# A planner's other durations and due times: one instruction stream of a state-space and attention block, put in another order

## The chip, the cores and the metric

The kernel runs on one core of one Trainium2 chip. The metric is the device time of one launch in microseconds (us). The kernel before took 3198.13 us, the median of three runs (3196.02 to 3198.74).

## What is computed

All tensors are 32-bit floats. The input `x` has 8 images of 384 channels by 32x32 places. Layer 0 is a Mamba block, run forwards and backwards over the 1024 places, joined by a gated depthwise 3x3 convolution. Layer 1 is causal attention over the 1024 tokens (key width 64) and a feed-forward layer of width 1536 whose weights are Kronecker products. Cut to what matters:

```python
# layer 0, per image; mamba() runs forwards and on the flipped sequence
u, z  = split(x_norm @ in_proj_w.T)
u     = silu(causal_conv4(u) + conv1d_b)
dt, Bm, Cm = split(u @ x_proj_w.T)
delta = softplus(dt @ dt_proj_w.T + dt_proj_b)
h     = exp(delta * A) * h + (delta * u) * Bm      # a scan over 1024 places, 384 x 16 states
y     = (sum_n h * Cm + u * D) * silu(z)
g     = (mamba(x) + flip(mamba(flip(x)))) @ out_proj_w.T * scale_mod
x     = x + res_scale * (g + sigmoid(conv3x3(x_norm) + dw_b) * x_norm)
# layer 1
t = t + softmax(causal(rope(n @ Wq) @ rope(n @ Wk).T / 8)) @ (n @ Wv)   # n = layernorm(t)
t = t + gelu(layernorm(t) @ w_fc.T) @ w_proj.T
```

## The kernel before, in words

The work on an image is cut along the sequence into two halves of 512 places (`HB`). There are four scan steps for each image (`STEPS`): direction 1 on half 1, then on half 0, then direction 0 on half 0, then on half 1. A scan step has 12 *units*: six groups of 64 channels by two groups of eight states. So there are 48 units for each image and 384 in all. `scan` writes one unit as follows:

- SP (SyncE's DMA queue) loads four 256 KB tiles of `dd` (delta, spread over the states) into `dl`, and four of `db` (delta times u) into a tile of `hs`. The `hs` tiles are 128x2048, and there are five of them; `dl` has five tiles of 128x512.
- POOL (GpSimd) multiplies the `hs` tile by `br` (the input coefficients).
- ACT (ScalarE) makes four exponentials `da`, each in a PSUM bank. There are three such banks.
- DVE (VectorE) runs four `tensor_tensor_scan` of 128x512. In half of the steps each takes its first value from `carry`, a small tile that ACT copies out of the last scan of an earlier step.
- DVE multiplies the tile by `cb` (the output coefficients). In four units of twelve (`POOL_C`) POOL does that, with `cr`.
- PE (TensorE) sums over the states with four matmuls into the PSUM bank `y`. After four units ACT or DVE takes `y` away.

Everything else is *side work*, written as generators in small pieces: the norm and the input projection (`norm_in`), the 1-d convolution (`conv_tokens`, in which SP loads four overlapping copies `rep` and PE multiplies them by `cwt`), delta and its products (`prepare`), the gate and the 3x3 convolution (`gate`, `conv`, `local`, with `rep` and `cit`), the output projection (`project`), attention and the feed-forward layer. Their PSUM banks are the two `w`.

None of these calls issues an instruction. Each engine object records the call (`Plan.add`), and `Plan.order` then decides the order of all of them by list scheduling. It plays the program through with its own figures: `add` gives every instruction a duration `cost` (lines 149 to 173), `order` keeps a clock for each engine, and at every step the engine that can start first takes, of its operations that are ready, the one of lowest `rank`. Rank is the due time less a bonus (`rush`), and due times are counted in units: image b begins at 48b. A piece of side work gets its due time from `spread`, between two times of a table (FIRST, SECOND and OTHERS for layer 0; LAYER1, LAYER1_6 and LAYER1_7 for layer 1). The operations of a unit get theirs from SCAN. Buffers are handed out in the same play. The result is one fixed order for each engine; on the chip each engine works it off in order and waits for what it needs.

Three more parts of the play matter below. A load's landing time (lines 393 to 395) is made of a common rate and a fixed part, and the sync queue's clock is held back when more than 9 us of transfers are queued (`AHEAD`). `_gated` models TensorE's clock in windows of 3.413 us, with a half rate after a window of little work. `_fill` puts matmuls of zeros (`y<-zero,ident` in the profile) into modelled holes of TensorE until the last window is busy for the share `KEEP`. So the number of these fillers depends on the durations too; all other instructions are fixed.

All instructions are issued in `issue`, so in the profile they carry line 423, and the activation tables line 421. They are told apart by tile names. A 32-bit matmul appears as two records.

Of the kernel before, what the change touches and what calls it, by code (L numbers as in the profile page):

```python
# [34 lines left out]
POOL_END = (1, 3, 6, 8, 10)  # L35
TMP, SIDE = 5, 4
REPS = 4
RUSH = 3.54
START, LATER = -40.0, -8.0
LATER_US = 36.0  # L40


FIRST = (1.62, 3.88, 10.08, 14.37, 18.13, 22.35)
SECOND = (23.0, 0.55)
OTHERS = (4.41, 9.05, 14.9, 16.09, 22.99, 26.51, 31.92, 33.87, 42.68, 49.8)
BURST = 8.0
PROJECT = 1.86
LAYER1 = (39.24, 51.32, 61.95, 72.21, 83.3)
LAYER1_6 = (40.54, 50, 58.1, 65.96, 73.04)
LAYER1_7 = (39.38, 43.03, 45.9, 58.42, 62.69, 67.55, 71.01, 75.01, 81.01)  # L50
HASTE = 22.72
FREE = ["w", "da", "cb", "w", "da", "cb", "da"]
EXPS = 0.0
SCAN = (-1.59, -1.1, -0.46, -0.4, -0.36, 0.15, 0.79, 1.19)
class _Op:


    __slots__ = (
        "eng", "call", "args", "kw", "due", "rush", "seq", "cost", "tail", "bytes", "table", "batch", "tiles", "rank",
        "busy", "early", "succ", "left", "ready", "preds", "issued",  # L60
    )


# [13 lines left out]
class Plan:  # L77
# [5 lines left out]
        AF.Exp: "natural_log_exp_and_others", AF.Ln: "natural_log_exp_and_others",  # L83
        AF.Softplus: "softplus", AF.Silu: "silu_and_others", AF.Tanh: "silu_and_others", AF.Gelu: "gelu_and_others",
    }
    SWITCH = 1.3
    LOOSE = ("w", "tmp", "side")
    HURRY = 7.31
    PATIENCE = 1.81
    SETTLE = 0.2  # L90
    HOP = 0.18
    RATE = 300e3
    LAND = 2.54
    GATE = 3.413
    WARM, COLD = 0.8, 0.45
    KEEP = 0.65
    AHEAD = 9.0
    FAR = 1 << 24

    def __init__(self, nc, tc):  # L100
# [38 lines left out]
    def add(self, eng, call, method, args, kw):  # L139
        op = _Op()  # L140
        op.eng, op.call, op.args, op.kw = eng, call, args, kw
        op.due, op.rush, op.early, op.seq = self.due, self.rush, self.early, len(self.ops)
        outs = [args[0]] + [v for k, v in kw.items() if k == "accum_out"]
        ins = [v for v in args[1:] if isinstance(v, bass.AP)]
        ins += [v for k, v in kw.items() if k != "accum_out" and isinstance(v, bass.AP)]
        op.tiles = [(t, True) for t in outs] + [(t, False) for t in ins]
        n = max(math.prod(t.shape[1:]) for t in (outs[0], ins[0]) if len(t.shape) > 1) if ins else 1
        op.tail, op.bytes = self.HOP, 0
        op.table, op.batch = None, self.batch
        if method == "dma_start":  # L150
            op.bytes = math.prod(outs[0].shape) * 4
            op.cost = 0.45 if eng == "sync" else 1.0
        elif eng == "tensor":
            once = kw.get("is_transpose") or method == "transpose"

            m = outs[0].shape[0]
            rate = 1.05 if once else 0.62 if m <= 32 else 1.0 if m <= 64 else 1.72
            op.cost = 0.02 + rate * max(n, 96) / 1e3
            op.busy = 0.75 if once else min(1.0, ins[0].shape[0] / 96)
            op.tail += self.SETTLE  # L160
        elif eng == "vector":
            scan = method == "tensor_tensor_scan"
            op.cost = 0.14 + (2.09 if scan else 1.04) * n / 1e3
            if method == "scalar_tensor_tensor":
                op.cost += 0.06
            if method in ("tensor_copy", "bn_aggr"):
                op.cost = 0.16
        elif eng == "scalar":
            aps = sum(1 for k, v in kw.items() if k in ("scale", "bias") and isinstance(v, bass.AP))
            op.cost = 0.21 + 0.714 * n / 1e3 + 0.05 * (method == "activation") + 0.06 * aps + 0.2 * ("accum_out" in kw)  # L170
            op.table = self.SETS.get(args[2]) if method == "activation" else self.set
        elif eng == "gpsimd":
            op.cost = (0.45 + 1.0 * n / 1e3) if len(ins) == 1 else (0.1 + 2.165 * n / 1e3)
        self.ops.append(op)

    def spread(self, gen, a, e):
# [90 lines left out]
    def _fill(self, t, now, begun):  # L267

        work = sum(b * (e - max(s, now - self.GATE)) for s, e, b in self.ran[-40:] if e > now - self.GATE)
        out, left, right = self.nothing  # L270
        n = right.shape[1]
        made = []
        while work < self.KEEP * self.GATE:
            op = _Op()
            op.eng, op.call, op.args = "tensor", self.nc.tensor.matmul, (out, left, right)
            op.kw = dict(start=not begun, stop=False, skip_group_check=True)
            op.cost, op.busy, op.bytes, op.table = 0.02 + 1.72 * n / 1e3, 1.0, 0, None
            op.due, op.tiles, op.batch = 0.0, (), None
            if t + op.cost > now:
                break  # L280
            made.append((t, op))
            work += self._gated(t, op) - t
            t = self.ran[-1][1]
        return made

    def order(self):
# [11 lines left out]
        clock = dict.fromkeys(engines, 0.0)  # L298
        cand = {e: [op for op in self.ops if op.eng == e and not op.left] for e in engines}
        table, kept = None, 0.0  # L300
        drained = 0.0
        batches, whole = {}, {}
        for op in self.ops:
            if op.batch is not None and op.table is not None:
# [50 lines left out]
        while issued < total:  # L355
            best = None
            for e in engines:
                ts = [(at(op), op) for op in cand[e]]
                ts = [(t, op) for t, op in ts if t is not None]
                if not ts:  # L360
                    continue
                now = max(clock[e], min(t for t, _ in ts))
                if best is None or now < best[0]:
                    best = (now, e, ts)
            assert best, "no instruction can start"
            now, e, ts = best

            op = min((op for t, op in ts if t <= now), key=lambda op: op.rank)
            issued += 1
            cand[e].remove(op)  # L370
            op.issued = True
            for name in op.tiles:
                if name in self.slot:
                    continue
                tag = tag_of[name]
                self.slot[name] = min(free[tag])[1]
                free[tag].remove(min(free[tag]))
                queue[tag].remove(name)
            cost = op.cost
            if op.table is not None and op.table != table:  # L380
                cost += self.SWITCH
                table = op.table
            if e == "tensor" and self.nothing and now > clock[e]:

                y = [name for name in left_y if name in self.slot and users[name]]
                begun = bool(y) and left_y[y[0]] not in (0, all_y[y[0]])
                if begun or not y and max([last[n] for n in left_y if n in last], default=0.0) < clock[e]:
                    started += self._fill(clock[e], now, begun)
            started.append((now, op))
            end = clock[e] = self._gated(now, op) if e == "tensor" else now + cost  # L390
            done = end + op.tail
            if op.bytes:
                drained = max(drained, end + 0.3) + op.bytes / self.RATE
                done = drained + self.LAND
                clock[e] = max(end, drained - self.AHEAD)
            if op.table is not None:
                kept, batch = end, op.batch
                if batch is not None:
                    batches[batch] -= 1
            for name in op.tiles:  # L400
                users[name] -= 1
                if name in left_y and e == "tensor":
                    left_y[name] -= 1
                last[name] = max(last.get(name, 0.0), done)
                if not users[name]:
                    free[tag_of[name]].append((last[name], self.slot[name]))
            for o in op.succ:
                o.left -= 1
                o.ready = max(o.ready, end if o.eng == e and not op.bytes else done)
                if not o.left:  # L410
                    cand[o.eng].append(o)
        self.started = started
# [14 lines left out]
def conv_attn_kernel(  # L427
# [520 lines left out]
    def scan(b, si, lo=0, hi=HB):  # L948
# [38 lines left out]
        for k in range(n_u):  # L987
# [3 lines left out]
            if g == 0:  # L991
# [20 lines left out]
                if part == 0:  # L1012
# [7 lines left out]
                    for sb, (_, src) in zip(held_in, parts):  # L1020
                        plan.sync.dma_start(sb, src)
                    plan.due, plan.rush = t + 0.5 * f, RUSH
                    y = plan.tile(ps_y, [P, HB], "y")[:, :n]
# [22 lines left out]
            if save:  # L1046
                plan.due, plan.rush = t + f * 0.6, RUSH
                plan.scalar.copy(carry[:, k], hs[:, :, 0 if d else n - 1])
# [4 lines left out]
            else:  # L1053
                plan.vector.tensor_mul(hs, hs, cb[g].unsqueeze(1).to_broadcast([P, NQ, n]))
            plan.due, plan.rush = t + f * SCAN[7], RUSH
            done = part == 1 and g == SG - 1
# [417 lines left out]
```

## Time and profile before

| | |
|---|---|
| runs | 3196.02, 3198.13, 3198.74 us |
| span of the profiled execution | 3199.6 us (its own run time is not given apart) |
| granted TensorE clock, mean | 0.964 |
| VectorE busy | 2675.7 us, of which scans 1820 us |
| GpSimd busy | 2693.5 us, of which 128x2048 products 2256 us |
| ScalarE busy | 2189.8 us, of which exponentials 1057 us and table loads 205 us |
| TensorE busy, with fillers | 2770.0 us, of which fillers 350 us (1304 records) |
| DMA | 762 MB, mean 238 GB/s |

A wait row of the profile has, after the arrow's releaser, the total in us, how often, and the longest. A group row has busy time and mean duration; "DMA issues" end in the median us from issue to landing. A row of a timeline begins with start and length in us. Busy time is the union of the records, and neighbouring records on one engine may overlap by some hundredths of a us.

### The profile page before, as it was taken

To read this page: it belongs to the slowest core of one execution; us is meant where nothing else is said; L and a number is where in the kernel's file an instruction comes from. 1 tells how busy PE (TensorE), PEld (TensorE's weight loads), DVE (VectorE), ACT (ScalarE), POOL (GpSimd) and SP (SyncE) were. 2 spreads that over 40 slices of the span, in tenths; PEclk is the share of its full clock that TensorE was granted. 3 is DMA by queue.
4 is the path that set the end of the run, shared out by engine and by line. 5 is a ranking of instruction groups with operands and counts; after the bars stand their busy time and mean duration, and the time that the engine had idled before them with its cause. 6 is when DMAs were issued, how large, how long until landed. Compare 5 with 4: busy or idle time off the path is not lost. (4 is left out here: it accounts for less than half of the span.)

```text
span 3199.6 us, 39939 instructions
## 1 busy us (share of the span) xinstructions
PE 2770.0 (87%) x11855; PEld 1160.9 (36%) x11855; DVE 2675.7 (84%) x2740; ACT 2189.8 (68%) x3591; POOL 2693.5 (84%) x923
## 2 busy tenths in 40 slices
PE   7887888888988989899888888898898998787789
PEld 3323333343333334343333433334343433343345
DVE  3778778897898889997899978988799979998972
ACT  3566676867677776868578676767768686666564
POOL 2888887788998889889889888888898989998950
PEclk9998999999999999999999998999999999999899
DMA  7998997878979887887978788798878879665530
GB/s 232 289 293 259 285 286 224 260 230 260 265 229 279 250 248 242 270 251 239 266 239 268 237 252 249 223 279 243 262 236 258 259 237 279 196 197 175 174 100 12
DMA packets 424462, 762.47 MB, mean 238 GB/s; under 512 B 51020, under 2 KB 70804, under 8 KB 424244
## 3 DMA queue, kind: packets, MB, share of 16 engines
q1 hardware_dynamic: 424116, 759.80, 78.5%
q8 instruction: 93, 1.52, 0.2%
q14 instruction: 125, 1.02, 0.1%
q0 software_dynamic: 128, 0.11, 0.0%
HBM read 617.92 MB, written 141.80 MB: 237 GB/s over the span
## 5 line engine op out<-in xcount | busy, mean ns | idle before, releaser
L423 POOL TENSOR_TENSOR hs<-hs,br 128x2048 f32<-128x2048 f32 (+1 forms) x395 | 1737.6, 4406 | 312.6 <-PE y L423 156.1
L423 ACT ACTIVATE da<-dl,nega 128x512 f32<-128x512 f32 (+1 forms) x1584 | 1056.6, 677 | 534.5 <-DVE hs L423 384.0
L423 DVE TENSOR_TENSOR_SCAN hs<-da,carry,hs 128x512 f32<-128x512 f32 (+1 forms) x816 | 935.7, 1201 | 125.1 <-ACT da L423 113.7
L423 DVE TENSOR_TENSOR_SCAN hs<-da,hs 128x512 f32<-128x512 f32 x768 | 883.9, 1202 | 132.6 <-ACT da L423 115.5
L423 POOL TENSOR_TENSOR hs<-hs,cr 128x2048 f32<-128x2048 f32 (+1 forms) x137 | 599.0, 4372 | 30.1 <-DVE hs L423 23.3
L423 DVE TENSOR_TENSOR hs<-hs,cb 128x2048 f32<-128x2048 f32 (+1 forms) x259 | 574.1, 2217 | 44.4 <-ACT carry L423 38.4
L423 PE MATMUL y<-hs,sel 128*32 128x512 f32 (+1 forms) x3168 | 446.7, 607 | 91.2 <-POOL hs L423 54.5
L423 PE MATMUL y<-zero,ident 128*128 128x256 f32 x1304 | 349.7, 398 | 0.0
L423 PEld LDWEIGHTS y<-zero,ident 128*128 128x128 f32 x1304 | 237.9, 195 | 144.7 <-issue 121.4
L423 PE MATMUL w<-rep,cit 96*32 96x512 f32 x1152 | 199.2, 657 | 34.1 <-DMA rep<-xq 26.3
L421 ACT ACT_TABLE_LOAD x160 | 205.3, 1283 | 2.8
L423 PE MATMUL w<-v,p 128*128 128x384 f32 x546 | 196.5, 506 | 10.4 <-ACT p L423 9.3
L423 PEld LDWEIGHTS y<-hs,sel 128*32 128x32 f32 x3168 | 80.9, 110 | 339.3 <-DVE hs L423 128.6
L423 PE MATMUL w<-q,fc1s 128*128 128x512 f32 (+1 forms) x388 | 191.0, 607 | 12.8 <-ACT p L423 6.0
L423 PE MATMUL w<-rep,cwt 128*32 128x512 f32 x744 | 162.1, 613 | 28.8 <-DMA rep<-up 13.6
L423 PE MATMUL w<-wout,side 128*128 128x384 f32 x378 | 146.4, 515 | 31.7 <-DVE side L423 22.3
L423 ACT ACTIVATE uc<-w,vec 128x512 f32<-128x512 f32 x144 | 97.1, 680 | 109.4 <-PE w L423 91.4
L423 ACT COPY gl<-w 128x512 f32<-128x512 f32 (+2 forms) x254 | 136.7, 549 | 23.4 <-PE w L423 21.2
L423 PE MATMUL w<-xn,wz 128*128 128x512 f32 x288 | 135.5, 614 | 11.3 <-ACT uc L423 5.0
L423 PEld LDWEIGHTS w<-v,p 128*128 128x128 f32 x546 | 101.4, 194 | 100.3 <-ACT p L423 31.2
L423 PE MATMUL w<-xn,win 128*128 128x512 f32 x288 | 133.5, 605 | 4.6 <-ACT tmp L423 4.4
L423 PE MATMUL w<-wvs,gl 128*128 128x384 f32 x372 | 135.4, 502 | 0.8 <-ACT uc L423 0.6
(204 smaller groups left out, 3191.8 us busy)
## 6 DMA issues: line engine op xcount, KB each, us to landing
dl<-dd SPq DMA_DIRECT2D x744, 256.0 KB, 5.4
hs<-db SPq DMA_DIRECT2D x744, 256.0 KB, 5.6
rep<-up SPq DMA_DIRECT2D x180, 257.5 KB, 6.4
rep<-xq SPq DMA_DIRECT2D x192, 222.4 KB, 7.1
tmp<-in_x_dram SPq DMA_DIRECT2D x96, 256.0 KB, 5.4
dd<-tmp SPq DMA_DIRECT2D x96, 256.0 KB, 3.7
db<-uc SPq DMA_DIRECT2D x96, 256.0 KB, 4.2
br<-bd SPq DMA_DIRECT2D x62, 256.0 KB, 5.8
```

Of the source, the lines that this page charges most:

```text
L421: self.nc.scalar.preload_act_table_set(table)
L423: op.call(*args, **{k: self._bind(v) for k, v in op.kw.items()})
```

## The change

The diff leaves all calls that record work as they are, and with that the instructions, apart from fillers and the number of table loads that the order needs. It changes four things.

It replaces the formulas by which `add` prices an instruction. It gives each engine its own delay until another engine sees its result (`TAIL`), and a delay of 0.07 us to a later instruction of the same engine, but not on TensorE (`RAW`). It changes the play of transfers: a new rate, a fixed part for each (`FIX`), a lead of 1.2 us from the issue (`LEAD`), half a us less for writes to DRAM, and for the sync queue, in place of `AHEAD`, a limit of eight transfers in flight (`LANES`). It sets the due times, bonuses and `KEEP` anew. `op.done` is stored and not read by the functions shown.

```diff
-RUSH = 3.54
+RUSH = 3.67
-FIRST = (1.62, 3.88, 10.08, 14.37, 18.13, 22.35)
-SECOND = (23.0, 0.55)
-OTHERS = (4.41, 9.05, 14.9, 16.09, 22.99, 26.51, 31.92, 33.87, 42.68, 49.8)
-BURST = 8.0
-PROJECT = 1.86
-LAYER1 = (39.24, 51.32, 61.95, 72.21, 83.3)
-LAYER1_6 = (40.54, 50, 58.1, 65.96, 73.04)
-LAYER1_7 = (39.38, 43.03, 45.9, 58.42, 62.69, 67.55, 71.01, 75.01, 81.01)
-HASTE = 22.72
+FIRST = (2.5, 3.88, 9.91, 14.33, 18.07, 21.68)
+SECOND = (22.97, 0.53)
+OTHERS = (4.59, 6.98, 14.9, 16.45, 23.04, 25.93, 32.33, 33.23, 40.61, 49.8)
+BURST = 6.85
+PROJECT = 2
+LAYER1 = (39.92, 51.24, 61.95, 70.76, 83.52)
+LAYER1_6 = (39.47, 49.56, 58.33, 65.89, 73.37)
+LAYER1_7 = (41.09, 42.02, 49.22, 58.28, 64.49, 67.56, 67.85, 73.12, 81.01)
+HASTE = 22.26
-EXPS = 0.0
-SCAN = (-1.59, -1.1, -0.46, -0.4, -0.36, 0.15, 0.79, 1.19)
+EXPS = 0.09
+SCAN = (-1.38, -0.85, -0.52, -0.39, -0.37, 0.12, 0.79, 1.19)
...
-    SWITCH = 1.3
+    SWITCH = 1.4
-    PATIENCE = 1.81
-    SETTLE = 0.2
-    HOP = 0.18
-    RATE = 300e3
-    LAND = 2.54
+    PATIENCE = 1.92
+    TAIL = dict(tensor=0.21, vector=0.117, scalar=0.14, gpsimd=0.1, sync=0.1)
+    RAW = 0.07
+    RATE = 320e3
+    LEAD, FIX, LAND = 1.2, 0.1, 2.8
+    LANES = 8
-    KEEP = 0.65
-    AHEAD = 9.0
+    KEEP = 0.67
...
         if method == "dma_start":
             op.bytes = math.prod(outs[0].shape) * 4
-            op.cost = 0.45 if eng == "sync" else 1.0
+            op.write = outs[0].space == bass.MemoryType.DRAM
+            op.cost = (0.45 if op.write else 0.62) if eng == "sync" else 0.8
         elif eng == "tensor":
             once = kw.get("is_transpose") or method == "transpose"
             m = outs[0].shape[0]
-            rate = 1.05 if once else 0.62 if m <= 32 else 1.0 if m <= 64 else 1.72
-            op.cost = 0.02 + rate * max(n, 96) / 1e3
+            rate = 0.85 if once else 0.43 if m <= 32 else 0.84 if m <= 64 else 1.676
+            op.cost = rate * max(n, 64) / 1e3
-            op.tail += self.SETTLE
         elif eng == "vector":
-            scan = method == "tensor_tensor_scan"
-            op.cost = 0.14 + (2.09 if scan else 1.04) * n / 1e3
+            if method == "tensor_tensor_scan":
+                op.cost = 2.0833e-3 * n + (0.108 if isinstance(args[3], bass.AP) else 0.048)
...
+            else:
+                op.cost = max(0.07, 0.048 + 1.0417e-3 * n + 0.06 * len(small))
         elif eng == "scalar":
-            op.cost = 0.21 + 0.714 * n / 1e3 + 0.05 * (method == "activation") + 0.06 * aps + 0.2 * ("accum_out" in kw)
+            op.cost = 0.05 + 0.8333e-3 * n + 0.05 * (not psum) + 0.095 * aps + 0.09 * ("accum_out" in kw)
         elif eng == "gpsimd":
-            op.cost = (0.45 + 1.0 * n / 1e3) if len(ins) == 1 else (0.1 + 2.165 * n / 1e3)
+            op.cost = 0.2 if n <= 16 else 0.2 + 2.5e-3 * n if len(ins) == 1 else 0.14 + 2.119e-3 * n
...
             if op.bytes:
-                drained = max(drained, end + 0.3) + op.bytes / self.RATE
-                done = drained + self.LAND
-                clock[e] = max(end, drained - self.AHEAD)
+                drained = max(drained, now + self.LEAD) + op.bytes / self.RATE + self.FIX
+                done = drained + self.LAND - 0.5 * op.write
+                if e == "sync":
+                    lanes = lanes[1:] + [done]
+                    clock[e] = max(end, lanes[0])
+            op.done = done
...
-                o.ready = max(o.ready, end if o.eng == e and not op.bytes else done)
+                near = o.eng == e and not op.bytes
+                o.ready = max(o.ready, end + (0.0 if e == "tensor" else self.RAW) if near else done)
```

In `_fill` the price of a filler goes from 0.02 + 1.72n/1000 to 1.676n/1000 us, with n = 256.

More of the change, by code (lines that the diff above doesn't have):

```diff
@@ L59 @@
         "eng", "call", "args", "kw", "due", "rush", "seq", "cost", "tail", "bytes", "table", "batch", "tiles", "rank",
-        "busy", "early", "succ", "left", "ready", "preds", "issued",
+        "busy", "early", "write", "done", "succ", "left", "ready", "preds", "issued",
     )
@@ L147, in add @@
         n = max(math.prod(t.shape[1:]) for t in (outs[0], ins[0]) if len(t.shape) > 1) if ins else 1
-        op.tail, op.bytes = self.HOP, 0
-        op.table, op.batch = None, self.batch
+        op.bytes, op.table, op.batch = 0, None, self.batch
+        op.tail = self.TAIL[eng]
+        small = [v for v in args[1:] if isinstance(v, bass.AP) and len(v.shape) == 2 and v.shape[-1] == 1]
+        psum = bool(ins) and ins[0].space == bass.MemoryType.PSUM
         if method == "dma_start":
             op.bytes = math.prod(outs[0].shape) * 4
-            op.cost = 0.45 if eng == "sync" else 1.0
+            op.write = outs[0].space == bass.MemoryType.DRAM
+            op.cost = (0.45 if op.write else 0.62) if eng == "sync" else 0.8
         elif eng == "tensor":
@@ L156, in add @@
             m = outs[0].shape[0]
-            rate = 1.05 if once else 0.62 if m <= 32 else 1.0 if m <= 64 else 1.72
-            op.cost = 0.02 + rate * max(n, 96) / 1e3
+            rate = 0.85 if once else 0.43 if m <= 32 else 0.84 if m <= 64 else 1.676
+            op.cost = rate * max(n, 64) / 1e3
             op.busy = 0.75 if once else min(1.0, ins[0].shape[0] / 96)
-            op.tail += self.SETTLE
         elif eng == "vector":
-            scan = method == "tensor_tensor_scan"
-            op.cost = 0.14 + (2.09 if scan else 1.04) * n / 1e3
[L164 to L167, printed above, removed]
+            if method == "tensor_tensor_scan":
+                op.cost = 2.0833e-3 * n + (0.108 if isinstance(args[3], bass.AP) else 0.048)
+            elif method == "bn_stats":
+                op.cost = 0.157 + 1.0417e-3 * n
+            elif method == "bn_aggr":
+                op.cost = 0.1
+            elif method == "memset":
+                op.cost = 0.06 + 0.5e-3 * n
+            else:
+                op.cost = max(0.07, 0.048 + 1.0417e-3 * n + 0.06 * len(small))
         elif eng == "scalar":
             aps = sum(1 for k, v in kw.items() if k in ("scale", "bias") and isinstance(v, bass.AP))
-            op.cost = 0.21 + 0.714 * n / 1e3 + 0.05 * (method == "activation") + 0.06 * aps + 0.2 * ("accum_out" in kw)
+            op.cost = 0.05 + 0.8333e-3 * n + 0.05 * (not psum) + 0.095 * aps + 0.09 * ("accum_out" in kw)
             op.table = self.SETS.get(args[2]) if method == "activation" else self.set
         elif eng == "gpsimd":
-            op.cost = (0.45 + 1.0 * n / 1e3) if len(ins) == 1 else (0.1 + 2.165 * n / 1e3)
+            op.cost = 0.2 if n <= 16 else 0.2 + 2.5e-3 * n if len(ins) == 1 else 0.14 + 2.119e-3 * n
         self.ops.append(op)
@@ L276, in _fill @@
             op.kw = dict(start=not begun, stop=False, skip_group_check=True)
-            op.cost, op.busy, op.bytes, op.table = 0.02 + 1.72 * n / 1e3, 1.0, 0, None
+            op.cost, op.busy, op.bytes, op.table = 1.676 * n / 1e3, 1.0, 0, None
             op.due, op.tiles, op.batch = 0.0, (), None
@@ L300, in order @@
         table, kept = None, 0.0
-        drained = 0.0
+        drained, lanes = 0.0, [0.0] * self.LANES
         batches, whole = {}, {}
```

## The prediction

> **What bounds the kernel now.** I read the busy shares first, then the stretches, then the waits.
>
> ```profile
> PE 2770.0 (87%) x11855; PEld 1160.9 (36%) x11855; DVE 2675.7 (84%) x2740; ACT 2189.8 (68%) x3591; POOL 2693.5 (84%) x923
> ```
> ```profile
> core 0: us, PE busy (x) PEld busy (x) DVE busy (x) ACT busy (x) POOL busy (x), PEclk, DMA share, GB/s
> 0.00:160.00 160.00, 130.09 (x418) 54.62 (x419) 83.77 (x118) 75.12 (x113) 87.55 (x48) 0.94 0.88 260
> 160.00:400.00 240.00, 194.00 (x792) 73.65 (x790) 192.76 (x159) 147.93 (x221) 210.36 (x67) 0.92 0.93 279
> 400.00:2800.00 2400.00, 2112.52 (x9128) 865.55 (x9132) 2105.53 (x2084) 1722.55 (x2783) 2130.10 (x709) 0.97 0.83 251
> 2800.00:3080.00 280.00, 224.04 (x1004) 104.11 (x996) 249.24 (x293) 177.65 (x342) 249.14 (x85) 0.92 0.58 177
> 3080.00:3200.00 120.00, 109.37 (x524) 62.92 (x520) 44.45 (x90) 66.59 (x136) 16.39 (x17) 1.00 0.08 25
> ```
>
> DVE and POOL share the bound, each with about 500 us of holes. In 400 to 2800 they stand idle 294 and 270 us of 2400; the rest lies mostly at both ends, where too little work is ready. An order can mend the holes only. The waits tell who is late:
>
> ```profile
> ACT da L423 <- DVE hs L423: 384.0, 485, 5.2
> DVE hs L423 <- ACT da L423: 229.2, 91, 6.8
> POOL hs L423 <- PE y L423: 156.1, 49, 10.5
> ACT da L423 <- DMA dl<-dd: 117.7, 87, 5.0
> ACT uc L423 <- PE w L423: 94.5, 61, 5.7
> ```
>
> The first is harmless: ScalarE is ahead and waits for one of three `da` banks. The second is the damage: 91 times a scan had no exponential. ScalarE was then itself held up at the head of its queue, by the two last lines among others: a `dl` tile that had not landed, or a convolution's accumulator that TensorE had not finished. The third is `hs` buffers that come free late.
>
> [...] exponentials stand 229.2 us behind other work while the scans starve. So a wrong place in the queue costs time, and the place comes from the planner's prices. [...] the trace shows 0.92 in 2800 to 3080, where TensorE was 80% busy. [...] mean durations are not the spacing; this case's timeline shows it (next part). [...] Landings of `dl` from 3.0 to 8.9 us at 83% busy DMA engines fit a part that grows with load; the constants have none.
>
> **The prices, part by part.** The spacing is in the timeline:
>
> ```profile
> 1193.51 8.33 DVE L423 TENSOR_TENSOR_SCAN hs<-da,carry,hs 128x512 f32<-128x512 f32 x7
> 1251.83 3.43 DVE L423 TENSOR_TENSOR_SCAN hs<-da,hs 128x512 f32<-128x512 f32 x3
> 1208.78 2.76 PE L423 MATMUL w<-rep,cit 96*32 96x512 f32 x24
> 1227.20 1.92 PE L423 MATMUL y<-hs,sel 128*32 128x512 f32 x16
> ```
> ```profile
> dl<-dd SPq DMA_DIRECT2D x744, 256.0 KB, 5.4
> hs<-db SPq DMA_DIRECT2D x744, 256.0 KB, 5.6
> rep<-up SPq DMA_DIRECT2D x180, 257.5 KB, 6.4
> rep<-xq SPq DMA_DIRECT2D x192, 222.4 KB, 7.1
> ```
>
> Seven scans with a carry take 8.33, one 1.26: spacing (8.33-1.26)/6 = 1.18 us. Without a carry (3.43-1.20)/2 = 1.115. Old price 1.21 for both, new 1.175 and 1.115. The multiply by `cb` starts at 1191.30 and its follower at 1193.51: 2.21; old 2.27, new 2.18. A matmul is two records: the 12 of a convolution take 2.76; old 4.04, new 2.64. Four y matmuls alone take 1.06 and eight 1.92, so four add 0.86; old 1.35, new 0.88. POOL's 128x2048 hardly moves (4.53 to 4.48; record 4.54). A 256 KB load lands, by price, after 0.45+0.3+0.87+2.54 = 4.16 old and 1.2+0.82+0.1+2.8 = 4.92 new, against 5.4 to 7.1. SP's issue of a load is 0.45 old, 0.62 new; the four in a row that a `rep` or `dl` set needs start 0.56 to 0.65 apart. The eight lanes are new; SP does wait for its own landings (151 times for `hs<-db`, 64.3 us), so there is something for them to model. In sum the new prices are nearer the spacing on every engine but POOL, where both are right.
>
> What that moves, row by row, against the profiled span of 3199.6 (1.5 us, 0.05%, above the median 3198.13; what lies around the span is not shown):
>
> 1. **Late `dl`.** The landing is under-priced by 5.4-4.16 = 1.24 us before and 0.48 after, so 0.76 us better. Over 87 waits 66 us of ScalarE. Three `da` banks (3 x 1.18 us) can hide one such wait, not a row of them: I take half, **-33**. Bounds 0 (the load waits for one of five `dl` buffers anyway: SP stands 285 us behind ACT `da`) and -66.
> 2. **Late convolutions.** The same 0.76 plus three later issues of 0.17 makes 1.27 us for the last `rep`. Over 61 waits 77 us; half, **-39**. Bounds 0 and -77.
> 3. **Cheaper TensorE.** Summed over the counts of the groups, real matmuls are priced at about 2390 us before and 1960 after. Less assumed delay of y moves POOL's 49 waits either way: 49 x 0.47 = 23 us, taken as 0, bounds -23 and +23. But `_fill` adds fillers wherever its picture of TensorE is less than 67% busy. There are 1304/2 = 652 now. The 430 us that leave the picture could be filled by up to 1000 more; I take 330. A filler takes about 0.44 us (ten records 2.34). If a quarter stand before a matmul that was ready on the chip, and cost half of it: 330/4 x 0.22 = **+18**. Bounds: 0 where the array is idle as planned, below zero by the clock (mean 0.964: at most 3.6% of the TensorE part of the chain, PE 6% of the span, 7 us), and +102 as in the rival below.
> 4. **Dues.** POOL's products and exponentials come due 0.21 and 0.25 of a unit later (SCAN), EXPS gives 0.09 back. A unit is 3199.6/384 = 8.3 us. An extra PSUM copy of 0.58 before the exponentials in a quarter of the units would be 96 x 0.58 = 56, half of it seen by DVE: +28. The other end is -28, where the copy was what held TensorE's banks. Taken 0. Norms (OTHERS) and projections (PROJECT) move by up to 2 units; these have a whole batch to be hidden in: 0, and if that cover fails a 1.8 us join per batch, 14.
> 5. **Ends.** The first 160 us are limited by loads (DMA share 0.88) and the last 120 by a serial chain with PE 109 us busy. LAYER1_7 moves dues by up to 3.3 units; an order can't shorten the chain: 0, bounds -12 and +12.
> 6. **Table loads** (160 x 1.283 us; SWITCH 1.3 to 1.4, PATIENCE +0.11): ten fewer or more are 13 us on an engine busy 68%: 0.
>
> Sum -33-39+18 = -54: 3199.6-54 = 3145.6; on the median's footing **3144**.
>
> **The rivals.** (a) *As summed*, 3109 to 3185, chance 0.50. (b) *The queues fit throughout*: with spacing priced right the scheduler lines up all engines, and not only loads. If half of POOL's middle waits go (PE y 153, `db` 35, issue 32: half of 220 is 110) the time is 3199-110 = 3089. For it: the near-exact prices. Against it: landings stay under-priced, and most PE y waits may be five `hs` buffers rather than order. Chance 0.20. (c) *Buffers set the loads, whatever the order*: rows 1 and 2 are zero, 3192 to 3204. For it SP's 285 us behind `da` and 301 us behind y. It is also the rival that the new order differs little where it matters. Chance 0.09. (d) *Fillers crowd TensorE*, ending slower: 700 more, a third of them whole in front of y or convolution matmuls, 233 x 0.44 = 102 us; y late means `hs` late and POOL idle, and with the gain of 72 the end is 3199+30 = 3229. It decides from about 165 such fillers on. For it: PE is 87% busy already and its y products stand on POOL's longest wait. Against: fillers are put only in modelled gaps, and real TensorE work is priced lower there because it is shorter. Chance 0.21.
>
> **How the numbers follow.** About 0.2% (6 us) is what a measurement of this kernel tells from no change. Faster: (a), (b) and 0.02 of (c) give 0.72; same 0.07 from (c); slower (d) 0.21. The range 3085 to 3225 holds (a), (c), about half of (b) and half of (d): 0.80. The likeliest case's own range is 3109 to 3185.
>
> **What would show it.** Right: DVE `hs` behind ACT `da` falls from 229 to about 160, `da` behind `dl` from 118 to about 60, `uc` behind PE from 94 to about 50, middle DVE idle below 260 us of 2400. Filler records rise from 1304 to near 1960. Wrong in steps 1 and 2: these rows stay, or shrink with no gain while POOL behind PE y grows. Wrong in step 3: fillers above 2700 and PE y above 200 us, or fewer fillers than now. The prediction fails altogether if the ends, and not the middle, move the time.

## The result: slower by 1.8%, and the profile after

The changed kernel took **3254.86 us** (median of 4; 3250.05 to 3261.27) against 3197.07 for the kernel before in the same sessions (median of 4). The ratio is 1.0177, interval 1.0154 to 1.02. The forecast of 3144 had the wrong sign. The profiled execution of the changed kernel has a span of 3248.3 us, 48.7 more than the one before.

The page's first part, and the stretch from 400 to 2800 us, to be set beside the same lines of before:

```profile
PE 2993.6 (92%) x12775; PEld 1312.7 (40%) x12775; DVE 2656.8 (82%) x2740; ACT 2178.3 (67%) x3589; POOL 2689.1 (83%) x923
```
```profile
400.00:2800.00 2400.00, 2272.66 (x9712) 975.35 (x9709) 2041.93 (x2030) 1685.19 (x2733) 2084.71 (x698) 1.00 0.84 249
```

DVE, ACT and POOL do the same work as before, so their busy times hardly move. TensorE has 224 us more. In the middle, DVE and POOL are 64 and 45 us less busy than before in the same 2400 us: most of the loss is there. (In the first 400 us DVE does another 16 us less work than before; some of all this is made up after 2800.) At the start of the last scan (3169.0 us, before 3116.3) the changed kernel is 53 us behind. The waits of the changed kernel (total us, times, longest):

```profile
ACT da L433 <- DVE hs L433: 282.6, 379, 4.3
DVE hs L433 <- ACT da L433: 248.3, 101, 12.1
POOL hs L433 <- PE y L433: 178.6, 52, 7.4
ACT uc L433 <- PE w L433: 159.9, 111, 6.9
ACT v L433 <- PE w L433: 64.4, 41, 3.4
ACT da L433 <- DMA dl<-dd: 58.6, 48, 5.5
```

The wait for late `dl` loads fell from 117.7 to 58.6 us, as forecast. But `uc` behind TensorE rose from 94.5 to 159.9, `v` from 26.4 to 64.4. Over all rows of ScalarE's waits, those for a DMA went from 185 to 92 us, and **those for TensorE from 263 to 486**. One wait was traded for a larger one. But ScalarE is not the bound, so what VectorE waits for counts more. Over the whole span its waits for ScalarE rose from 307 to 343 us, over all rows, and its own **waits for TensorE from 111 to 171** (of these, 52 to 106 between 400 and 2800). The rows behind TensorE that grew most, first before, then after:

```profile
DVE side L423 <- PE y L423: 31.4, 14, 3.7
DVE p L423 <- PE w L423: 14.4, 3, 9.2
DVE q L423 <- PE w L423: 13.4, 10, 3.7
DVE sm L423 <- PE w L423: 11.7, 5, 5.3
```
```profile
DVE p L433 <- PE w L433: 39.0, 10, 7.4
DVE side L433 <- PE y L433: 38.7, 25, 4.4
DVE sm L433 <- PE w L433: 38.3, 33, 3.6
DVE q L433 <- PE w L433: 22.6, 14, 3.7
```

These are VectorE's parts of the gate and of layer 1. So more of the added idle time of VectorE comes straight from TensorE (60 us) than through ScalarE (36). Two groups of the page show what TensorE does with its extra time:

```profile
L433 PE MATMUL y<-zero,ident 128*128 128x256 f32 x2224 | 582.3, 393 | 0.0
...
L433 PE MATMUL w<-rep,cwt 128*32 128x512 f32 x744 | 219.8, 610 | 2.8 <-DMA rep<-up 1.9
```

There are 1112 fillers (2224 records) for 652, and the same 372 matmuls of the 1-d convolution take 219.8 us, before 162.1.

### The profile page after: what moved, and what is told of

The parts are those of the page before. It is cut to its first block, busy times and chain, and to the rows that moved or that the text cites. A ratio compares the mean times of both kernels' runs of the same rounds, so it can differ in the third digit from the quotient of the medians.

```text
span 3248.3 us, 41611 instructions
## 1 busy us (share of the span) xinstructions
PE 2993.6 (92%) x12775; PEld 1312.7 (40%) x12775; DVE 2656.8 (82%) x2740; ACT 2178.3 (67%) x3589; POOL 2689.1 (83%) x923
## 5 line engine op out<-in xcount | busy, mean ns | idle before, releaser
L433 POOL TENSOR_TENSOR hs<-hs,br 128x2048 f32<-128x2048 f32 (+1 forms) x395 | 1737.1, 4407 | 339.0 <-PE y L433 178.6
L433 DVE TENSOR_TENSOR_SCAN hs<-da,hs 128x512 f32<-128x512 f32 x768 | 886.7, 1204 | 156.1 <-ACT da L433 135.7
L433 PE MATMUL y<-zero,ident 128*128 128x256 f32 x2224 | 582.3, 393 | 0.0
L433 PE MATMUL y<-hs,sel 128*32 128x512 f32 (+1 forms) x3168 | 473.9, 600 | 98.5 <-POOL hs L433 55.1
L433 PEld LDWEIGHTS y<-zero,ident 128*128 128x128 f32 x2224 | 398.2, 191 | 259.4 <-issue 218.7
L433 PE MATMUL w<-rep,cwt 128*32 128x512 f32 x744 | 219.8, 610 | 2.8 <-DMA rep<-up 1.9
```

What stands on the lines that cost most here:

```text
L433: op.call(*args, **{k: self._bind(v) for k, v in op.kw.items()})
```

## Where the price is wrong

The old and the new price of a 32-column matmul are flat numbers, 0.337 and 0.22 us for an input of 128x512. Two pieces of TensorE's timeline, first of the kernel before, then of the changed one (start, length, records; two records are one matmul):

```profile
401.91 0.59 PE L423 MATMUL w<-rep,cwt 128*32 128x512 f32 x1
402.19 0.59 PE L423 MATMUL y<-hs,sel 128*32 128x512 f32 x1
402.34 0.59 PE L423 MATMUL w<-rep,cwt 128*32 128x512 f32 x1
```
```profile
436.12 2.56 PE L433 MATMUL w<-rep,cwt 128*32 128x512 f32 x12
438.62 0.70 PE L433 MATMUL y<-zero,ident 128*128 128x256 f32 x2
439.25 1.91 PE L433 MATMUL w<-rep,cwt 128*32 128x512 f32 x4
441.08 1.13 PE L433 MATMUL y<-side,ddiag 128*128 128x512 f32 x2
```

The two records of the convolution are 0.43 apart, so one matmul takes 0.86 by itself; here a record of y runs beside it. In the changed kernel six matmuls hold TensorE 2.50 us to the next start, 0.42 each; a filler stands between them and the last two; these hold it 1.83, **0.92 each**. The 3x3 convolution of 12 shown in the prediction had 0.23 each. The difference is the neighbour. In `conv_tokens` a set of four matmuls writes four different groups of 32 columns, one for each `rep` tile, while the two matmuls that one `rep` tile feeds (one for each direction) write the same group in two banks. Of the y run at 1227.20 us in the kernel before, the first four records start within 0.02 us, the first eight, those of four matmuls, within 0.47, and the next four matmuls begin 0.88 after the first. So in this trace partners on other columns are nearly free (0.88 us for four, 0.86 for one by itself), and a matmul without them costs a whole one. Four at 0.22 are right as a set and wrong one by one. When the four `rep` loads land one after another, the planner plays each matmul at 0.22, puts fillers or other work in between, and believes that TensorE is free four times sooner than it is.

The traces show how often that happens. Counting unbroken runs of the 1-d convolution on TensorE, the kernel before has 20 runs of eight matmuls and 4 runs of only two; the changed kernel has 3 of eight and **65 of two**. A run of two takes 1.83 us in the median there, 0.92 for each matmul, and a run of four 1.00, 0.25 for each. Of the 65, 48 have a filler right before or behind them. So the low price made the planner break up the sets that the low price needs.

Counted from the starts of the records (an instruction holds TensorE until the next start, or for its length less the 0.16 us by which neighbours overlap), all real matmuls held TensorE 2305 us before and 2312 after. So the real work took as long as before. The planner's prices for it, added up over every matmul of the two programs, are 2453 us before and 2008 after (the prediction's count by groups gave 2390 and 1960): 6% too high and 13% too low. Part of the held time passed at a half clock (the granted clock of the traces is 1 or 0.5, and was 0.5 for 229 us of the span before and 113 after), for which the planner adds by itself; counted at the full clock it is 2216 and 2279, and the sums are 11% too high and 12% too low. So by its sum neither table is the nearer one. They miss on opposite sides. The 372 matmuls of the 1-d convolution are priced at 125 us before and 82 after, and held TensorE 140 and 182.

## The experiments

Medians are over the runs of each kernel; the ratio is to the kernel before on the same chip. Beside the runs of the experiments the kernel before took 3196 to 3204 us. The last two columns are from the profiles: fillers (half the records), and ScalarE's waits for TensorE over all rows.

| kernel | us | ratio, interval | fillers | ACT waits for PE, us |
|---|---|---|---|---|
| before | 3197 | 1 | 652 | 263 |
| changed | 3255 | 1.0177 (1.0154, 1.0200) | 1112 | 486 |
| a_half | 3230 | 1.0082 (1.0062, 1.0101) | 556 | 450 |
| a_none | 3289 | 1.0267 (1.0247, 1.0287) | 0 | 503 |
| prices | 3347 | 1.0456 (1.0424, 1.0488) | 1150 | 505 |
| dues | 3229 | 1.0088 (1.0067, 1.0108) | 686 | 307 |
| a_pe | 3251 | 1.0160 (1.0136, 1.0183) | 638 | 276 |
| a_dma | 3291 | 1.0287 (1.0265, 1.0310) | 1069 | 491 |
| a_eng | 3293 | 1.0291 (1.0273, 1.0309) | 1149 | 495 |
| b_narrow | 3280 | 1.0250 (1.0204, 1.0296) | 862 | 391 |
| b_shift1 | 3248 | 1.0144 (1.0110, 1.0179) | 662 | 308 |
| a_shift1 | 3302 | 1.0317 (1.0276, 1.0358) | 1163 | 523 |
| a_later | 3327 | 1.0388 (1.0353, 1.0423) | 1112 | 444 |
| b_more | 3220 | 1.0064 (1.0039, 1.0090) | 1108 | 286 |
| b_pe | 3360 | 1.0514 (1.0494, 1.0535) | 1101 | 496 |
| a_pe_shift1 | 3248 | 1.0162 (1.0142, 1.0183) | 614 | 291 |
| a_pack | 3219 | 1.0081 (1.0052, 1.0111) | 923 | 355 |
| a_shift1_half | 3251 | 1.0178 (1.0157, 1.0199) | 582 | 471 |
| a_pack_half | 3243 | 1.0135 (1.0114, 1.0157) | 462 | 370 |
| b_less | 3210 | 1.0025 (1.0011, 1.0039) | 456 | 272 |

**First: fillers, prices or dues?** The theory was the prediction's rival (d), surplus fillers (F); against it the order of the real instructions (O), the dues (D), or a mixture of dues and prices that do not fit (M). `a_half` and `a_none` keep the changed order and only drop fillers where it is handed on (the diff is `a_none`'s; `a_half` leaves out every second one):

```diff
-        return [op for _, op in started]
+        return [op for _, op in started if not isinstance(op.tiles, tuple)]
```

> The changed kernel with its order kept, and every second filler matmul left out (about 556 left instead of 1112; before has 652; a filler multiplies zeros, so nothing that is computed is left out). Theory F (the added fillers delay TensorE): the time falls from 3255 most of the way back, to 3190-3225, ScalarE's uc wait for TensorE from 160 us to about 110, and POOL's wait for y from 179 to about 160. Theory O (the order of the real instructions is the cause): within 10 us of 3255. A third possibility is a drop of the granted clock that gives back what the fillers took.

> The changed kernel with its order kept and all fillers left out (nothing that is computed is left out). Theory F with a cheap clock: 3160-3200. Theory F with a costly clock: granted clock under 0.85 and 3220-3300, so that the fillers are needed. Theory O: 3245-3265 if the clock matters little.

Half of the fillers gone won 25 us, a little less than half of the loss and short of F's 3190 to 3225. `uc` behind TensorE fell to 129 us, not to 110; the other waits hardly moved. With none the granted clock falls to 0.902 (0.983 changed; the mark was 0.85) and the time rises to 3289. So F is right in part: the surplus costs, some fillers are needed, and some 30 us are left in this order that the count of fillers does not explain. `prices` is the changed kernel with the constants from RUSH to SCAN of before; `dues` is the reverse:

> The new prices, play of transfers, SWITCH, PATIENCE and KEEP, with the due times and bonuses of before. Theory F: the fillers come with the prices, so slower than before by at least 30 us, 3230-3260. Theory D (the dues set anew are what costs): 3190-3205. Theory M (the dues were fitted to the prices they stand with, and a mixture is worse than either): over 3265.

> The old prices and the old play with the due times and bonuses of the change. Theory F: 3190-3215, with about 650 fillers. Theory D: 3240-3260. Theory M: over 3215 with fillers as before.

Each half alone is slower than before, and prices alone are worst: 3347. The new dues take back about 90 of those 150 us, yet on the old prices they lose 0.88%, 28 us. So M holds, and the new prices look like the harmful half.

**Second: which price?** One group at a time is set back:

```diff
 # a_pe
-            rate = 0.85 if once else 0.43 if m <= 32 else 0.84 if m <= 64 else 1.676
-            op.cost = rate * max(n, 64) / 1e3
+            rate = 1.05 if once else 0.62 if m <= 32 else 1.0 if m <= 64 else 1.72
+            op.cost = 0.02 + rate * max(n, 96) / 1e3
-    TAIL = dict(tensor=0.21, ...
+    TAIL = dict(tensor=0.38, ...
...
 # b_narrow, in the kernel before
-            rate = ... 0.62 if m <= 32 else 1.0 if m <= 64 ...
+            rate = ... 0.40 if m <= 32 else 0.82 if m <= 64 ...
```

`a_dma` takes back the transfers and SP's prices, `a_eng` the formulas of VectorE, ScalarE and GpSimd with their delays:

```diff
 # a_dma
-    RATE = 320e3
-    LEAD, FIX, LAND = 1.2, 0.1, 2.8
+    RATE = 300e3
+    LAND, AHEAD = 2.54, 9.0
-            op.cost = (0.45 if op.write else 0.62) if eng == "sync" else 0.8
+            op.cost = 0.45 if eng == "sync" else 1.0
...
 # a_eng
-    TAIL = dict(tensor=0.21, vector=0.117, scalar=0.14, gpsimd=0.1, sync=0.1)
-    RAW = 0.07
+    TAIL = dict(tensor=0.21, vector=0.18, scalar=0.18, gpsimd=0.18, sync=0.18)
+    RAW = 0.0
...
```

> The changed kernel with TensorE's prices and its delay (0.38 us) of before, fillers' price included; the rest new. Theory P (TensorE priced too low: a 32-column matmul costs 0.22 only where its partners run beside it, and about 0.98 alone; so ScalarE's copies stand too early in its queue and fillers go in between partners): back to 3185-3215, fillers 600-800, ScalarE's waits for TensorE in all from 486 us to under 320. Theory Q (another price, or any new order is a draw): 3235-3270 or worse.

> The changed kernel with the play of transfers and SP's prices of before; the rest new. Theory P: no better than the change, 3245-3290, and ScalarE's wait for dl loads from 59 us back over 100. Theory T (the transfers' new play, with its eight lanes, is what costs): 3190-3220.

> The changed kernel with the prices and delays of VectorE, ScalarE and GpSimd of before and no RAW; the rest new. Theory P: 3240-3290, ScalarE's waits for TensorE still over 400 us. Theory E (the cheaper scans and exponentials are what costs): 3190-3220.

> The kernel before with one price changed: matmuls of 32 columns at 0.225 us for 512 (before 0.337) and of 64 at 0.44; all else as before, dues too. Theory P: slower than before, 3215-3260, fillers up from 652 to about 800, ScalarE's waits for TensorE from 263 us to over 350. Theory Q: any value, with no tie to ScalarE's waits for TensorE. If this price does nothing: 3190-3207.

TensorE's prices did to the fillers and to ScalarE's waits exactly what theory P said (638 and 276 us), and P's time failed: 3251, not 3185 to 3215. Taking back any other group left the waits at 490 and made the kernel slower. The lower price for 32 and 64 columns alone, put into the kernel before, cost 2.5% (more than P's 3260) and raised the waits to 391. That *every* edit lost to the kernel before spoke for theory Q, that a new order is a draw.

**Third: how much is a draw?** In `b_shift1` and `a_shift1` each due time of the side work moves by 0.05 of a unit, up or down by chance, with no price changed:

```diff
-OTHERS = (4.41, 9.05, 14.9, 16.09, 22.99, 26.51, 31.92, 33.87, 42.68, 49.8)
+OTHERS = (4.46, 9.10, 14.85, 16.04, 23.04, 26.46, 31.97, 33.92, 42.63, 49.85)
...
```

> The kernel before with each due time of FIRST, OTHERS and the LAYER1 tables moved by 0.05 of a unit (0.4 us), up or down at random; prices as before. Theory Q (the list scheduler is chaotic, and before is a picked draw: any other order, for whatever reason, is a worse one): clearly slower than before, 3215-3260. Theory P (the time follows from the prices): within 10 us of before, 3190-3207.

> The changed kernel with the same shifts of 0.05 of a unit. Theory Q: the changed kernel is picked too, so slower than it, 3270-3310. If the changed kernel isn't a pick: as likely faster as slower, 3225-3285. Theory P: within 10 us of 3255.

Shifts of 0.4 us cost 1.4% in either kernel. Both stand some 47 us below this neighbour, so each is better fitted than an arbitrary set of dues near it (one draw each, so the size is rough). It follows that no mixture can be compared with either kernel, only with other unfitted orders. Sorted so, the draws fall apart by **TensorE's price**: with the old one 3229 (`dues`), 3248 and 3251; with the new one 3291, 3293, 3302 and 3347. `b_narrow`, with only the narrow prices lowered, stands between them at 3280, so of its 2.5% more than half may be the lost fit.

`a_later` tried the reverse cure: other engines keep their order, and in some 460 places a copy out of a `w` bank changes places with the exponential behind it. `b_more` keeps the order of before and doubles seven of ten fillers:

```diff
 # a_later, over the finished order; j is ScalarE's next instruction
+                if banks and not held and any(tag_of[n] == "da" for n in nxt.tiles) and fits(i, nxt):
+                    line.insert(i, line.pop(j))
...
 # b_more
...
+            if isinstance(op.tiles, tuple):
+                n += 7
+                if n >= 10:
+                    n -= 10
+                    kept.append(op)
```

> The order of the changed kernel, with one thing moved: on ScalarE's queue, in 461 places where a copy out of a PSUM bank w stands right ahead of an exponential, the two change places; all other engines keep their order. Theory P (the copies stand too early for TensorE): ScalarE's waits for TensorE fall from 486 us to 250-350, and the time by 15 to 45 us, 3210-3240. If the place of the copies is not what costs: waits fall, but TensorE now waits for its banks and the time stays within 10 us of 3255 or rises.

> The order of the kernel before with seven of ten fillers doubled, at the places where they stand: about 1108 in place of 652, as many as the changed kernel has. Theory F (fillers by themselves cost about what half of the changed kernel's cost, 25 us): 3215-3235. If fillers in planned gaps are free, or win by the clock: 3185-3205.

`a_later` lost 72 us. ScalarE's waits for TensorE fell only to 444, and TensorE's waits for ScalarE rose from 101 to 168. So to move the copies alone, with TensorE's order kept, is no cure; whether their place is a part of the cause this doesn't settle. `b_more` lost 19 us: as many fillers as in the changed kernel cost that much in a fixed order.

**Fourth: the level, and what in the price.** `b_pe` puts TensorE's new prices and delay into the kernel before (the reverse of `a_pe`'s diff), `a_pe_shift1` is a second unfitted order with the old ones. `a_pack` changes one thing in the changed kernel: a 32-column matmul costs a whole one when it starts alone.

```diff
...
+            if not once and m <= 32:
+                op.cols = outs[0].offset % self.FAR // outs[0].ap[0][0] // 32
+                op.cost = 1.676 * max(n, 64) / 1e3
...
+            if e == "tensor":
+                if op.cols is None or now > clock[e] + 1e-6 or op.cols in pack:
+                    pack.clear()
+                elif pack:
+                    op.cost = 0.015
+                if op.cols is not None:
+                    pack.add(op.cols)
```

> The kernel before with TensorE's prices and delay (0.21 us) of the change, fillers' price included; all else as before. Level theory (unpicked orders under the new TensorE prices stand at 3290-3350, under the old ones at 3230-3250): 3280-3340, about 1100 fillers, ScalarE's waits for TensorE 450-530 us. Draw theory (any unpicked order is one draw from one spread, 3229-3347): as likely under as over 3270.

> The changed kernel with TensorE's prices and delay of before, and all due times shifted by 0.05 of a unit: a second unpicked order of that kind beside a_pe (3251). Level theory: 3225-3265, ScalarE's waits for TensorE under 320 us. Draw theory: anywhere from 3229 to 3347.

> The changed kernel with one price changed: a 32-column matmul costs 0.858 us for 512 when it starts alone, and 0.015 when it follows a partner on other columns at once; wide matmuls and the delay as in the change. If the flat 0.22 is what misleads the planner: 3225-3265 (an unpicked order), ScalarE's waits for TensorE under 350 us. If it is the general level of TensorE's prices and its delay, or the fillers: 3285-3340 and waits over 430 us.

> The order of the shifted changed kernel (3302) with every second filler left out (about 580 of 1163 left). Theory F: faster by 15 to 35 us, 3267-3287, as in a_half. If a_half's gain was particular to its order: within 10 us of 3302.

The levels stand: `b_pe` 3360 (even above its 3340), `a_pe_shift1` 3248. Means over the unfitted orders are 3244 (four, old) and 3319 (five, new), 75 us apart with no overlap. `a_pack`, with TensorE's other new prices and the new delay, came out at 3219, better than the changed kernel that is fitted to the flat price, and 100 us under the mean of its level. Its runs of two convolutions are down from 65 to 5, and its runs of eight up from 3 to 15; over all orders that have fillers, TensorE's old prices give 4 to 8 runs of two, the new flat ones 24 to 65, and `b_narrow` 13. The planner's prices in `a_pack` sum to 2217 us, against 2268 held at the full clock.

One thing besides the price moves here. `spread` shares out due times by the prices, and the whole price for each single matmul shifts those of 2592 of the 15691 instructions, by 0.16 of a unit in the median. That is more than the shifts of 0.05 that cost 47 us. So `a_pack` is one unfitted draw, and a lucky share of its 100 us can't be excluded; that its sets are whole again is read from the trace. Its waits, in rows that stand beside those of the changed kernel:

```profile
ACT uc L445 <- PE w L445: 86.6, 62, 7.2
ACT da L445 <- DMA dl<-dd: 61.5, 57, 7.7
ACT tmp L445 <- PE w L445: 51.9, 66, 3.4
ACT v L445 <- PE w L445: 45.9, 36, 5.6
```
```profile
L445 PE MATMUL w<-rep,cwt 128*32 128x512 f32 x744 | 179.8, 608 | 32.6 <-DMA rep<-up 26.8 <-ACT uc L445 4.3 <-DVE t L445 0.6
```

`uc` behind TensorE is back under its value of before (86.6 for 94.5), the convolution falls from 219.8 to 179.8 (before 162.1), and the gain on `dl` is kept (61.5). ScalarE's waits for TensorE are 355, a little over the 350 expected.

In the shifted order half of the fillers were worth 51 us, more than the 15 to 35 expected. That brings it to 3251, as low as the unfitted orders with the old price, although ScalarE still waits 471 us for TensorE (`a_pe`, also 3251, has 276). So in this order surplus fillers may be nearly the whole difference between the levels, and ScalarE's total wait doesn't tell the time. Fewer fillers also close up sets: the 41 runs of two in `a_shift1` become 25. But the count of fillers is not enough either: `a_pack` has 923 of them at 3219, `b_narrow` 862 at 3280. The reading that fits is that it matters whether the gap that a filler is put into exists; no run separates this from the broken sets.

The last two asked whether still fewer fillers would beat both kernels. `a_pack_half` drops every second filler of `a_pack`. `b_less` was meant to drop seven of ten of the kernel before; its edit keeps seven of ten and drops three, so that 456 are left (912 records), not 196.

```diff
 # b_less
+            if isinstance(op.tiles, tuple):
+                n += 7
+                if n < 10:
+                    continue
+                n -= 10
+            kept.append(op)
```

> The order of a_pack with every second filler left out (about 460 of 923 left). If fillers keep costing as in a_half: 3185-3205, at or under the kernel before. If under some 600 fillers the clock gives back what they took: 3205-3230.

> The order of the kernel before with seven of ten fillers left out (about 196 of 652 left). If fillers cost at every count: 3175-3190, faster than before. If the clock needs them at this count: granted clock under 0.94 and 3200-3235.

Neither did: 3243, slower than either forecast, and 3210. What 196 fillers would do in the order of before was not measured. No kernel of the study beat the kernel before.

## Why the prediction was wrong, point by point

- **The premise that failed** is the sentence "In sum the new prices are nearer the spacing on every engine but POOL, where both are right", and with it the reason against rival (d), that real TensorE work "is priced lower there because it is shorter". The sentence holds for the scans, multiplies and transfers that were read. For TensorE I had read the price from one convolution and one y run whose partners stood together (0.23 and 0.22). One by one such a matmul holds TensorE 0.92, and in all the real work stayed at 2305 and 2312 us while its price fell from 2453 to 2008.
- **Steps 1 and 2, the way to the scans.** Both steps take half of a wait of ScalarE as won for VectorE, and the trace gives no ground for the half. Of the 229.2 us in which scans of the kernel before waited for `da`, ScalarE was busy for 215: 88 with side work, 70 with table loads, 57 with exponentials. It stood waiting for a load for 8 us and for TensorE for 5, of 118 us behind `dl` and 94 of `uc` behind TensorE in all. An earlier wait can still have pushed later work back, so this is not the whole of their effect; but what mostly stood before the late exponentials was other work in ScalarE's queue. In the changed kernel the 248.3 us are 103, 49 and 60, then 1 for loads and 33 for TensorE.
- **Step 1, late `dl`.** The wait itself moved as I said: "about 60", it is 58.6. The bound "0" was the better value for the time, for another reason than I gave: ScalarE's total wait went from 990 to 1049 us, since TensorE's lateness took the place.
- **Step 2, late convolutions.** Wrong sign. `uc` behind TensorE was to fall to about 50 and rose to 160. TensorE's waits for `rep<-up` did fall (13.6 to 1.9 us), so the loads came in time and the matmuls did not. In `a_pack` the row is 86.6.
- **Step 3, cheaper TensorE.** "I take 330" fillers; it was 460. "**+18**" for them; dropping half of all won 25 (`a_half`) and 51 (`a_shift1_half`), and the same surplus cost 19 in the order of before. What the step lacked is the effect of the low price on the places of real work: broken sets, and fillers in gaps that aren't there. The unfitted level is 75 us higher. The 23 us for POOL behind y, taken as 0, came at its upper bound (156.1 to 178.6).
- **Step 4, dues, "Taken 0"**, bounds 28. `dues` shows +28, `b_shift1` +47 for shifts of 0.4 us. A change of dues without a refit cost 1 to 1.5% in the three orders tried (`dues`, `b_shift1`, `a_shift1`). That the dues of both kernels are fitted to their prices is the reading that fits these three. I had priced single moves, not the loss of the fit.
- **Step 5, ends:** the last scan is 52.6 us late, the end 48.7: 4 us won, inside the bound of 12. In the first 160 us VectorE does 5 us and GpSimd 11 us less work than before. **Step 6:** 158 table loads for 160, nothing.
- **Rival (d)** had the right side and 3229. Its mark, POOL behind y above 200 us, did not come (178.6), nor 700 fillers. It named a part of the cause, the fillers. The range reached to 3225, 30 us short: it left out that the new order could be worse by its places.
- **What stays open:** how the 75 us divide between fillers and broken sets, which come together. A part goes straight to VectorE: over the whole span its waits for TensorE are 101 to 112 us in the four unfitted orders with the old price, 162 to 206 in the five with the new one, and 152 in `a_pack`. A refit of the dues to `a_pack`'s prices was not tried.

## What to carry to other kernels

A price in a list scheduler must be the price that the instruction has in the places where the scheduler will put it. A mean over well-packed sets invites the scheduler to break the sets up. So check a new price table against the time for which the trace shows the engine held, in all its work and not in its best rows; and look at the side on which it misses. Here a table 11% too high left TensorE some slack, and one 12% too low promised gaps that did not exist. And before a wait is counted as won, look at what the waited-for engine was doing: here ScalarE was hardly ever idle while the scans waited for it. When due times are fitted to a price table, a comparison of tables must be made between orders that are fitted alike: here 0.4 us of shift moved the time by 1.4%, nearly as much as the whole change.

## What the runs showed of the hardware

A matmul of a 128x512 input onto 32 columns held TensorE 0.92 us where its partners were away and 0.22 in the y run of eight. Of the counts of fillers tried, a middle one was best in two orders (the clock is that of the profiled run, the time the median): in the changed order 0, 556 and 1112 of them gave a clock of 0.902, 0.957 and 0.983 and times of 3289, 3230 and 3255. In the order of before 456, 652 and 1108 gave 0.954, 0.964 and 0.975, and 3210, 3197 and 3220. In `a_pack` more was better: 462 gave 0.951 and 3243, 923 gave 0.975 and 3219. In the kernel before, the granted clock was 0.5 from 480.11 us on for 3.41 us, after as long a stretch in which TensorE was busy for 1.45 us; TensorE was busy throughout at the half clock, and the next 3.41 us had the full one.

A 256 KB load into `dl` landed in the kernel before after a median of 4.2 us where the DMA share was 0.58 (2800 to 3080 us), 5.4 where it was 0.83 (400 to 2800) and 5.9 where it was 0.93 (160 to 400).
